# A new order for the token-only end of a two-layer metaformer kernel, with the FFN's fp8 casts on GpSimd

## The chip, the cores and the metric

The kernel runs on one core of a Trainium2 chip. A core has five engines with queues of their own: TensorE (PE, matrix products), VectorE (DVE), ScalarE (ACT), GpSimd (POOL) and SyncE (SP, which issues the transfers here). Each works through its own queue in order and waits for the others by semaphores. The metric is the device time of one execution in microseconds (us). One tick, below, is one turn of the kernel's main loop.

## The reference

The input `x` is 8 images of 128 x 128 pixels with 96 channels, in f32. Two layers follow one another. Each layer does

```python
x = x + conv(layernorm(x))      # eps 1e-6
t = x as tokens
t = t + ffn(layernorm(t))       # eps 1e-5
```

`conv` is a spectral filter: a product with `w1` to 192 channels, a squared ReLU, a two-dimensional real FFT, a product with a filter that is mixed for each image out of three learned ones by a small gate, the inverse FFT, and a product with `w2` back to 96 channels.

`ffn` is where the change is. With `q_mul` rounding to fp8 (5 exponent bits, 2 mantissa bits, overflow to infinity) and `q_acc` rounding to f16:

```python
def _qlinear(x, W, b):
    y = q_acc(jnp.einsum('bsk,nk->bsn', q_mul(x), q_mul(W)))
    return q_acc(y + q_mul(b))
h = jax.nn.relu(_qlinear(x, W1, b1))    # 96 -> 384
y = _qlinear(h, W2, b2)                 # 384 -> 96
```

So the normalised tokens are cast to fp8, the 384 hidden values are rounded to f16, biased, cut at zero and cast to fp8 again before the second product.

## The kernel before

The 2 x 8 pairs of layer and image are 16 jobs, and each job is cut into 16 groups, so every stage runs 256 groups (`n = NRG * len(jobs)`). There are four stages, written as Python generators whose `yield`s cut them into steps:

- `P`, `pixels`: loads 8 rows of pixels, normalises, multiplies by `w1`, squares, and does the first Fourier transform, along the width; the result goes to DRAM.
- `G`, `gate`: once per image, the mix of the three filters.
- `F`, `frequencies`: the transform along the height for 4 columns of frequencies, the filter, the product with `w2`, the inverse along the height; to DRAM.
- `S`, `tokens`: the inverse along the width for 8 rows, the residual, the layernorm, the FFN, the second residual, the store.

A fifth entry, `N`, does the small arithmetic of the layernorms: step 0 on VectorE (variance), step 1 on ScalarE (a logarithm and an exponential, for the inverse root), step 2 on VectorE (a refinement, and the bias of the normalisation).

No scheduler decides the order. A loop over ticks `t` walks through a tuple written by hand; an entry `(stage, step, ahead)` lets that step of the group `t - offset[stage] + ahead` be issued, with offsets 0 for P and G, 19 for F and 40 for S. Three tuples take turns: `RAMP` at the start, `TICK` for the body, and `TAIL` from the tick on at which only tokens are left (`t > n + offset["F"]`, that is from t = 276). At t = 276 the step with `ahead` 0 belongs to group 236, so some 20 groups of tokens remain for the tail. Each engine gets its instructions in the order of the tuple, and the loop goes on for as many ticks after the last group as the deepest step of `TAIL` lies behind (`last`). PSUM is four double banks, and `BANKS` and `TAIL_BANKS` say which tile takes which.

The steps of `tokens`, by number, with the name of the tile that the profile shows and the line in the kernel before:

| step | engine | what |
|---|---|---|
| 0 | SP | loads `v` (L742) and the residual `xr` (L744), 3 and 5 buffers |
| 1 | PE | `ps_r`, inverse transform (L748) |
| 2 | DVE | `xr` += `ps_r` (L757), 8 `bn_stats` (L371) |
| 3, 4 | DVE, ACT | normalise rows 0 to 3 and rows 4 to 7 into `xn_c`, fp8 (L772 on DVE, L766 on ACT) |
| 5 | PE | `pt_c`, 8 transposes (L780) |
| 6 | ACT | `xq`, the transposed tokens to SBUF (L783) |
| 7, 11, 15 | PE | `pm0`, `pm1`, `pm2`: a third of the 384 hidden values each (L790) |
| 8, 12, 16 | ACT | `y16`, `pm` to f16 (L793) |
| 9, 13, 17 | DVE | `a16`, bias and ReLU in f16 (L796) |
| 10, 14, 18 | ACT or POOL | `h8`, the fp8 cast of `a16` (L800 on ACT, L802 on POOL) |
| 19 | PE | `po`, second product, 24 matmuls (L807) |
| 20, 21 | ACT, DVE | `o16`, to f16 (L816), plus the bias (L818) |
| 22 | POOL, SP | `y` = `xr` + `o16` (L821), the store (L822) |

Which half of the rows ScalarE normalises is in `NORM_ACT`: `(1,)` means rows 4 to 7. Which of the three casts ScalarE makes is in `CAST_ACT`: `(0, 1, 2)` means all, and those that are not in it go to GpSimd.

Of the kernel before, what the change touches and what calls it, by code (L numbers as in the profile page):

```python
# [40 lines left out]
LAG = 3  # L41
WE = M + SC

NORM_ACT = (1,)
CAST_ACT = (0, 1, 2)
XS_ACT = (0, 1)


# [21 lines left out]
)  # L70

TAIL = (
    ("S", 5, -1), ("S", 14, -2), ("S", 15, -2), ("S", 6, -1), ("S", 2, 0), ("S", 7, -1),
    ("S", 16, -2), ("S", 19, -3), ("N", 0, 0), ("S", 8, -1), ("N", 1, 0), ("S", 20, -3),
    ("S", 17, -2), ("S", 9, -1), ("N", 2, 0), ("S", 3, 0), ("S", 21, -3), ("S", 10, -1),
    ("S", 11, -1), ("S", 22, -4), ("S", 12, -1), ("S", 0, 1), ("S", 1, 1), ("S", 4, 0),
    ("S", 13, -1), ("S", 18, -2),
)


# [6 lines left out]
    "pm1": 0, "pm2": 1, "po": 3, "pf2": 2, "py2": 0, "pz2": 2,  # L87
}
TAIL_BANKS = {
    "ps_r": 3, "pt_c": 1, "pm0": 1, "pm1": 2, "pm2": 2, "po": 3,  # L90
}

LAYER_INS = (
# [74 lines left out]
def _bc_mid(ap, n):  # L168

    p, a = ap.shape  # L170
    return ap.unsqueeze(1).to_broadcast([p, n, a])
# [3 lines left out]
def metaformer_kernel(ctx: ExitStack, tc: tile.TileContext, x, cst, layers, out):  # L175
# [5 lines left out]
    pp = ctx.enter_context(tc.tile_pool(name="psum", bufs=1, space=PSUM))  # L181

    banks = dict(BANKS, ps_w=0)

    def bank2(name):
        return pp.tile([128, 2, 512], F32, name=name, tag=f"d{banks[name]}")
# [165 lines left out]
    def rows(ap, g):  # L352
        return ap.rearrange("w (s h) c -> w s h c", s=2)[:, :, g * RH : (g + 1) * RH, :]
# [385 lines left out]
    def tokens(jb, g):  # L739
        wt = jb.wt  # L740
        v = ab.tile([128, RH, 2, C], F32, name="v", bufs=3)
        nc.sync.dma_start(v, jb.y[:, g * RH : (g + 1) * RH])  # L742
        xr = ab.tile([128, 2, RH, C], F32, name="xr", bufs=5)
        nc.sync.dma_start(xr, rows(jb.src, g))  # L744
        yield
        pr = bank2("ps_r")
        for s in range(2):
            mm(  # L748
                pr[:, s, : RH * C].rearrange("p (h c) -> p h c", c=C),
                kt["idft"],  # L750
                v[:, :, s, :],
                start=True,
                stop=True,
            )
        yield
        xv = xr.rearrange("p s h c -> p s (h c)")
        nc.vector.tensor_tensor(xv, pr[:, :, : RH * C], xv, ALU.add)  # L757
        x8 = xr.rearrange("p s h c -> p (s h) c")
        nm = norms[-1].stats(1, x8)
        yield  # L760

        xn = ab.tile([128, RG, C], F8, name="xn_c")
        for h in range(2):
            for j in range(RH * h, RH * h + RH):
                if h in NORM_ACT:
                    nc.scalar.activation(  # L766
                        xn[:, j, :], x8[:, j, :], AF.Identity,
                        bias=nm.nb[:, 1, j : j + 1], scale=nm.rs[:, 1, j : j + 1],
                        saturate=False,
                    )  # L770
                else:
                    nc.vector.tensor_scalar(  # L772
                        xn[:, j, :], x8[:, j, :], nm.rs[:, 1, j : j + 1], nm.nb[:, 1, j : j + 1],
                        ALU.mult, ALU.add, saturate=False,
                    )
            yield
        pt = bank2("pt_c")[:C]
        for j in range(RG):
            o = pt[:, j // 4, (j % 4) * 128 : (j % 4 + 1) * 128]
            mm(o, xn[:, j, :], ident8, start=True, stop=True)  # L780
        yield
        xq = ab.tile([C, 2, 512], F8, name="xq")
        nc.scalar.activation(xq, pt, AF.Copy, saturate=False)  # L783
        yield
        h8 = ab.tile([128, 3, 1024], F8, name="h8")
        for k in range(3):
            pm = bank2(f"pm{k}")
            fk = wt["f1_q"][:, k * 128 : (k + 1) * 128]
            for s in range(2):
                mm(pm[:, s, :], fk, xq[:, s, :], start=True, stop=True)  # L790
            yield
            y16 = ab.tile([128, 2, 512], F16, name="y16", bufs=3)
            nc.scalar.copy(y16, pm)  # L793
            yield
            a16 = ab.tile([128, 2, 512], F16, name="a16", bufs=3)
            nc.vector.tensor_scalar(a16, y16, wt["b1"][:, k : k + 1], 0.0, ALU.add, ALU.max)  # L796
            yield
            hk = h8[:, k, :].rearrange("p (a b) -> p a b", a=2)
            if k in CAST_ACT:
                nc.scalar.activation(hk, a16, AF.Copy, saturate=False)  # L800
            else:
                nc.gpsimd.tensor_copy(hk, a16, saturate=False)  # L802
            yield
        po = bank2("po")
        for j in range(RG):
            for k in range(3):
                mm(  # L807
                    po[:, j // 4, (j % 4) * C : (j % 4 + 1) * C],
                    h8[:, k, j * 128 : (j + 1) * 128],
                    wt["f2_q"][:, k, :],  # L810
                    start=k == 0,
                    stop=k == 2,
                )
        yield
        o16 = ab.tile([128, RG, C], F16, name="o16")
        nc.scalar.copy(o16.rearrange("p (a b) c -> p a (b c)", a=2), po[:, :, : RH * C])  # L816
        yield
        nc.vector.tensor_tensor(o16, o16, _bc_mid(wt["b2"], RG), ALU.add)  # L818
        yield
        y = ab.tile([128, 2, RH, C], F32, name="y")  # L820
        nc.gpsimd.tensor_tensor(y.rearrange("p s h c -> p (s h) c"), x8, o16, ALU.add)  # L821
        nc.sync.dma_start(rows(jb.dst, g), y)  # L822
        yield
# [6 lines left out]
    jobs = [Job(l, b) for l in range(len(layers)) for b in range(B)]  # L830
    first, last = max(a for _, _, a in RAMP), -min(a for _, _, a in TAIL)
    at, given, norms = {}, {}, []
    n = NRG * len(jobs)

    def advance(stage, step, last):

        for i in range(given.get((stage, step), 0), last + 1):
            if (stage, i) not in at:
                if stage == "N":
                    at[stage, i] = norms[i].steps()  # L840
                else:
                    at[stage, i] = stages[stage](jobs[i // NRG], i % NRG)
            next(at[stage, i])
            given[stage, step] = i + 1

    offset["N"] = -first
    with tc.manual_schedule():
        for t in range(-first, n + offset["S"] + last + 1):
            norms.append(Norms())
            if t < offset["F"] - 4:  # L850
                order, places = RAMP, RAMP_BANKS
            elif t > n + offset["F"]:
                order, places = TAIL, TAIL_BANKS
            else:
                order, places = TICK, BANKS
            banks.update(places)
            for stage, step, ahead in order:
                i = t - offset[stage] + ahead
                advance(stage, step, i if stage == "N" else min(i, n - 1))
# [40 lines left out]
```

## Time and profile before

| | before |
|---|---|
| time, median of 3 runs | 5379.85 us (5355.16 to 5381.69) |
| span of the profiled execution | 5367.8 us |
| TensorE, VectorE, ScalarE, GpSimd busy | 95%, 83%, 82%, 49% |
| mean granted TensorE clock | 0.974 of full speed |
| last `y` of the body's order (L821) | starts at 5134.6 us |
| last `y` of all | starts at 5362.5 us |

A line of a group reads: line, engine, operation, what is written from what, the sizes (partitions x elements) and types, how many; then, after the bar, the busy time in us and the mean of one in ns; then the time that the engine sat idle just before such instructions and what ended it. Busy time counts overlapping instructions once, so it can be less than the number times the mean. In the timeline, a line starts with the start in us and the duration in us.

The tail is the last 230 us or so of 5368, about 4% of the execution. It is the only part in which the instructions of the two kernels differ.

### The profile page before, as it was taken

Reading aid. Unit: us, or ns where it says so; the run is one execution under the profiler, and the core shown is the slowest. Engines: PE = TensorE matmul, PEld = TensorE weight load, DVE = VectorE, ACT = ScalarE, POOL = GpSimd, SP = SyncE. Lnnn points to the kernel's source line nnn. Section 1 sums busy time; section 2 is a strip of 40 time slices with the busy share of each in tenths; the row PEclk is TensorE's granted clock in tenths of the full one; section 3 lists DMA queues with packets and bytes.
Section 4 is the critical chain, followed back from the end, with each engine's and each line's share of the span. In section 5 each row is a group of like instructions: output and inputs, shape, how many; then the busy total and the mean of one; then the engine's idle time right before and its main releaser. Section 6 shows DMA issues by size and latency. Waiting matters only on the chain.

```text
span 5367.8 us, 116350 instructions
## 1 busy us (share of the span) xinstructions
PE 5075.2 (95%) x41192; PEld 4013.8 (75%) x41192; DVE 4474.8 (83%) x13814; ACT 4420.0 (82%) x7149; POOL 2651.8 (49%) x1911
## 2 busy tenths in 40 slices
PE   4899999999999999999999999999999999999876
PEld 2577777878787787878778787877878787787753
DVE  3887888888888888888888888888888888888876
ACT  2754688989898898989889898988989898897788
POOL 0355555555555555555555555555555555554421
PEclk7999999999999999999999999999999999999987
DMA  5566677777677777767777676777777677776643
GB/s 145 164 161 161 179 202 197 207 194 211 184 208 197 201 203 194 210 181 208 204 196 208 189 208 191 208 203 201 203 194 212 184 207 203 198 200 177 179 124 108
DMA packets 908040, 1020.14 MB, mean 190 GB/s; under 512 B 67106, under 2 KB 839954, under 8 KB 907122
## 3 DMA queue, kind: packets, MB, share of 16 engines
q1 hardware_dynamic: 907460, 1012.71, 68.3%
q8 instruction: 327, 5.36, 0.4%
q14 instruction: 253, 2.07, 0.1%
HBM read 598.62 MB, written 413.84 MB: 189 GB/s over the span
## 4 chain that ended last, share of the span: by engine, by line
PE 76%; DVE 8%; issue 6%; POOL 4%; ACT 3%; DMA 1%; SPq 1%; POOLq 0%; DVEq 0%; ACTq 0%
PE pw L458 13%; PE py L629 13%; PE pf L616 7%; PE pz L705 7%; PE pz L700 6%; PE pa L488 6%; PE pi L719 6%; PE ps_r L748 5%; PE pm L790 5%; PE pt_a L447 4%; PE po L807 3%; PE pt_c L780 2%; POOL ut L596 1%; DVE pr L647 1%; POOL y L821 1%
## 5 line engine op out<-in xcount | busy, mean ns | idle before, releaser
L659 POOL TENSOR_TENSOR xf<-pr 128x768 f32<-128x768 f32 (+2 forms) x544 | 957.0, 1762 | 312.5 <-DVE pr L651 278.0
L821 POOL TENSOR_TENSOR y<-xr,o 128x768 f32<-128x768 f32 x256 | 458.8, 1792 | 976.4 <-DVE o L818 940.8
L458 PE MATMUL pw<-w,xT 97*128 97x240 f32 x4096 | 925.1, 369 | 13.2 <-ACT xT L450 12.0
L443 POOL TENSOR_TENSOR xn_a<-xt,n_rs 128x768 f32<-128x768 f32 x256 | 413.6, 1616 | 976.8 <-DVE n_rs L409 852.8
L647 DVE TENSOR_TENSOR pr<-py,cf 128x768 f32<-128x768 f32 (+2 forms) x544 | 502.4, 924 | 465.6 <-PE py L629 422.8
L458 PEld LDWEIGHTS pw<-w,xT 97*128 97x128 f32 x4096 | 765.4, 192 | 136.4 <-ACT xT L450 22.8
L629 PE MATMUL py<-k_fwd,al 128*128 128x128 f32 x6272 | 838.9, 283 | 0.0
L793 ACT CAST y<-pm 128x1024 f16<-128x1024 f32 x768 | 770.8, 1005 | 58.3 <-PE pm L790 57.5
L800 ACT ACTIVATE h<-a 128x1024 fp8e5<-128x1024 f16 x768 | 808.3, 1055 | 0.4 <-DVE a L796 0.4
L629 PEld LDWEIGHTS py<-k_fwd,al 128*128 128x128 f32 x6272 | 751.1, 193 | 42.4 <-issue 7.3
L461 ACT ACTIVATE r<-pw 128x960 f32<-128x960 f32 x512 | 495.9, 969 | 280.1 <-PE pw L458 273.1
L596 POOL TENSOR_TENSOR ut<-ut,rw 112x768 f32<-112x768 f32 (+1 forms) x256 | 489.0, 1910 | 327.9 <-DMA ut<-u_d 177.7
L700 PE MATMUL pz<-w2b,xf 128*128 128x192 f32 (+1 forms) x2112 | 553.9, 344 | 8.8 <-DVE hr L534 5.0
L790 PE MATMUL pm<-xq,f_q 96*128 96x512 fp8e5 x1536 | 472.9, 390 | 71.7 <-ACT xq L783 39.7
L700 PEld LDWEIGHTS pz<-w2b,xf 128*128 128x128 f32 (+1 forms) x2112 | 337.7, 190 | 184.6 <-issue 143.1
L796 DVE TENSOR_SCALAR a<-y,b 128x1024 f16<-128x1024 f16 x768 | 434.2, 565 | 46.5 <-ACT y L793 46.5
L616 PEld LDWEIGHTS pf<-k_rh,ut 48*128 48x128 f32 x6272 | 376.8, 189 | 124.8 <-issue 65.1
L616 PE MATMUL pf<-k_rh,ut 48*128 48x128 f32 x6272 | 432.4, 284 | 36.9 <-POOL ut L596 35.8
L636 ACT COPY cf<-pf 128x768 f32<-128x768 f32 (+2 forms) x544 | 400.1, 796 | 36.2 <-PE pf L616 36.2
L465 ACT ACTIVATE xs<-r 128x768 f32<-128x768 f32 x512 | 427.6, 835 | 0.6
L783 ACT ACTIVATE xq<-pt_c 96x1024 fp8e5<-96x1024 f32 x256 | 260.7, 1018 | 184.0 <-PE pt_c L780 184.0
L719 PE MATMUL pi<-zt,k_inv 128*128 128x384 f32 (+1 forms) x1024 | 407.6, 522 | 0.0
(124 smaller groups left out, 10577.4 us busy)
## 6 DMA issues: line engine op xcount, KB each, us to landing
a_d<-at SPq DMA_DIRECT2D x256, 768.0 KB
al<-a_d SPq DMA_DIRECT2D x960, 192.0 KB
v<-y_d SPq DMA_DIRECT2D x256, 384.0 KB
y_d<-yt SPq DMA_DIRECT2D x480, 192.0 KB
ut<-u_d SPq DMA_DIRECT2D x240, 336.0 KB
xt<-in_x_dram SPq DMA_DIRECT2D x512, 96.0 KB
xr<-in_x_dram SPq DMA_DIRECT2D x128, 384.0 KB
mid<-y SPq DMA_DIRECT2D x128, 384.0 KB
```

What stands on the lines that cost most here:

```text
L458: mm(o, xT[:, 4 * a + 2 * i + j, :], wt["w1"], start=True, stop=True)
L596: nc.gpsimd.tensor_tensor(ut[:, :n], ut[:, :n], _bc_mid(jb.rw, n), ALU.mult)
L616: mm(pf[:nm, i, t * 128 : (t + 1) * 128], utf[64 * i : 64 * i + NHS, cs], kt["rh"][64 * i : 64 * i + NHS, :], start=True, stop=True,)
L629: mm(py[:nm, t, e, :], alf[:, e, cs], kt["fwd"][:, e, :], start=True, stop=True)
L647: nc.vector.tensor_tensor(p0, yq, crb, ALU.mult)
L659: nc.gpsimd.tensor_tensor(xv[:q, te], pr[:q, 0, te].rearrange("p t r k -> p t (r k)"), pr[:q, 1, te].rearrange("p t r k -> p t (r k)"), AL ...
L700: mm(o[:, : u * C], xf[:kb, 1, e, :], wt["w2b"][:kb, : u * C], start=True, stop=False,)
L719: mm(pi[:, e, : n * C], kt["inv"][:, e, :], zt[:, e, : n * C], start=True, stop=True)
L790: mm(pm[:, s, :], fk, xq[:, s, :], start=True, stop=True)
L793: nc.scalar.copy(y16, pm)
L800: nc.scalar.activation(hk, a16, AF.Copy, saturate=False)
L821: nc.gpsimd.tensor_tensor(y.rearrange("p s h c -> p (s h) c"), x8, o16, ALU.add)
```

## The change

From the tick on at which only tokens are left, GpSimd makes the three fp8 casts of the FFN instead of ScalarE, and ScalarE normalises all eight rows, of which VectorE did four. The order of the tail and its PSUM banks are written anew to go with it: for a group, `xq` now follows in the same tick as its normalisation, the residual and the statistics of a group are made one tick earlier, the pieces of a group lie at most three ticks apart and no longer four, and `pm0` and `pm1` share a bank while `pt_c` has one of its own. The purpose is to take work off ScalarE in the tail, where GpSimd has little to do. Before the tail, the two kernels issue the same instructions. What is computed is the same.

```diff
--- before.py
+++ after.py
@@ -41,8 +41,10 @@
 LAG = 3
 WE = M + SC
 
-NORM_ACT = (1,)
-CAST_ACT = (0, 1, 2)
+
+
+NORM_ACT, NORM_ACT_TAIL = (1,), (0, 1)
+CAST_ACT, CAST_ACT_TAIL = (0, 1, 2), ()
 XS_ACT = (0, 1)
 
 
@@ -70,11 +72,11 @@
 )
 
 TAIL = (
-    ("S", 5, -1), ("S", 14, -2), ("S", 15, -2), ("S", 6, -1), ("S", 2, 0), ("S", 7, -1),
-    ("S", 16, -2), ("S", 19, -3), ("N", 0, 0), ("S", 8, -1), ("N", 1, 0), ("S", 20, -3),
-    ("S", 17, -2), ("S", 9, -1), ("N", 2, 0), ("S", 3, 0), ("S", 21, -3), ("S", 10, -1),
-    ("S", 11, -1), ("S", 22, -4), ("S", 12, -1), ("S", 0, 1), ("S", 1, 1), ("S", 4, 0),
-    ("S", 13, -1), ("S", 18, -2),
+    ("N", 1, -1), ("S", 16, -2), ("S", 19, -3), ("N", 2, -1), ("S", 7, -1), ("S", 20, -3),
+    ("S", 8, -1), ("S", 1, 1), ("S", 17, -2), ("S", 21, -3), ("S", 9, -1), ("S", 18, -2),
+    ("S", 3, 0), ("S", 22, -3), ("S", 10, -1), ("S", 4, 0), ("S", 11, -1), ("S", 2, 1),
+    ("S", 12, -1), ("N", 0, 0), ("S", 5, 0), ("S", 6, 0), ("S", 13, -1), ("S", 14, -1),
+    ("S", 0, 2), ("S", 15, -1),
 )
 
 
@@ -87,7 +89,7 @@
     "pm1": 0, "pm2": 1, "po": 3, "pf2": 2, "py2": 0, "pz2": 2,
 }
 TAIL_BANKS = {
-    "ps_r": 3, "pt_c": 1, "pm0": 1, "pm1": 2, "pm2": 2, "po": 3,
+    "ps_r": 3, "pt_c": 1, "pm0": 0, "pm1": 0, "pm2": 2, "po": 3,
 }
 
 LAYER_INS = (
@@ -181,6 +183,7 @@
     pp = ctx.enter_context(tc.tile_pool(name="psum", bufs=1, space=PSUM))
 
     banks = dict(BANKS, ps_w=0)
+    on_act = {}
 
     def bank2(name):
         return pp.tile([128, 2, 512], F32, name=name, tag=f"d{banks[name]}")
@@ -762,7 +765,7 @@
         xn = ab.tile([128, RG, C], F8, name="xn_c")
         for h in range(2):
             for j in range(RH * h, RH * h + RH):
-                if h in NORM_ACT:
+                if h in on_act["norm"]:
                     nc.scalar.activation(
                         xn[:, j, :], x8[:, j, :], AF.Identity,
                         bias=nm.nb[:, 1, j : j + 1], scale=nm.rs[:, 1, j : j + 1],
@@ -796,7 +799,7 @@
             nc.vector.tensor_scalar(a16, y16, wt["b1"][:, k : k + 1], 0.0, ALU.add, ALU.max)
             yield
             hk = h8[:, k, :].rearrange("p (a b) -> p a b", a=2)
-            if k in CAST_ACT:
+            if k in on_act["cast"]:
                 nc.scalar.activation(hk, a16, AF.Copy, saturate=False)
             else:
                 nc.gpsimd.tensor_copy(hk, a16, saturate=False)
@@ -830,6 +833,7 @@
     jobs = [Job(l, b) for l in range(len(layers)) for b in range(B)]
     first, last = max(a for _, _, a in RAMP), -min(a for _, _, a in TAIL)
     at, given, norms = {}, {}, []
+    on_act.update(norm=NORM_ACT, cast=CAST_ACT)
     n = NRG * len(jobs)
 
     def advance(stage, step, last):
@@ -851,6 +855,7 @@
                 order, places = RAMP, RAMP_BANKS
             elif t > n + offset["F"]:
                 order, places = TAIL, TAIL_BANKS
+                on_act.update(norm=NORM_ACT_TAIL, cast=CAST_ACT_TAIL)
             else:
                 order, places = TICK, BANKS
             banks.update(places)
```

## The prediction

> **What bounds the kernel now.** I read the page first: ScalarE 82%, VectorE 83%, TensorE 95%, GpSimd 49%, all averages over a body that the change leaves alone. The list TAIL is in force only once pixels, gate and frequencies have run out, so I went on to busy time by stretch for the last 221 us (columns: stretch, its length, then busy us and instructions for PE, PEld, DVE, ACT, POOL, then clock and DMA).
>
> ```profile
> 5147.00:5181.00 34.00, 24.08 (x138) 13.70 (x138) 23.10 (x88) 28.48 (x46) 5.04 (x3) 0.80 0.38 118
> 5181.00:5344.00 163.00, 112.47 (x717) 65.06 (x715) 124.34 (x460) 154.38 (x240) 27.83 (x17) 0.83 0.37 119
> 5344.00:5367.80 23.80, 11.19 (x84) 7.44 (x84) 5.60 (x8) 14.30 (x19) 6.54 (x4) 0.50 0.18 67
> ```
>
> In the middle stretch 17 token groups pass (17 POOL instructions, one y each), so a tick is 163/17 = 9.59 us. ScalarE is busy 154.4/163 = 95%, GpSimd 17%. The groups of that stretch say what fills ScalarE:
>
> ```profile
> L800 ACT ACTIVATE h<-a 128x1024 fp8e5<-128x1024 f16 x52 | 53.0, 1051 | 0.0
> L793 ACT CAST y<-pm 128x1024 f16<-128x1024 f32 x52 | 51.3, 1005 | 1.4 <-PE pm L790 1.2
> L766 ACT ACTIVATE xn_c<-xr,n_nb,n_rs 128x96 fp8e5<-128x96 f32 x68 | 26.2, 463 | 0.0
> L783 ACT ACTIVATE xq<-pt_c 96x1024 fp8e5<-96x1024 f32 x17 | 17.1, 1007 | 0.0
> L816 ACT CAST o<-po 128x768 f16<-128x768 f32 x17 | 13.5, 794 | 6.7 <-PE po L807 6.6
> L796 DVE TENSOR_SCALAR a<-y,b 128x1024 f16<-128x1024 f16 x51 | 37.9, 743 | 33.9 <-ACT y L793 33.9
> L772 DVE TENSOR_SCALAR xn_c<-xr,n_rs,n_nb 128x96 fp8e5<-128x96 f32 x68 | 17.8, 325 | 0.6
> ```
>
> The fp8 casts (L800) are ScalarE's largest item. It idles only 0.5 us a tick, mostly for po; the others wait for it. So ScalarE bounds the tail.
>
> The a16 step deserves a second look: the groups give it 743 ns, but its own view has a median of 480 and a maximum of 5401, and the timeline shows why.
>
> ```profile
> L796 DVE TENSOR_SCALAR a<-y,b x768: 470/480/5401, 636.2 to 5356.9; 128x1024 f16<-128x1024 f16 x192
> ...
> 5314.99 1.64 POOL L821 TENSOR_TENSOR y<-xr,o 128x768 f32<-128x768 f32 x1 [8.32 <-DVE o L818]
> 5315.86 1.05 DVE L796 TENSOR_SCALAR a<-y,b 128x1024 f16<-128x1024 f16 x1 [0.95 <-ACT y L793]
> ```
>
> It began while GpSimd's y ran and ended at 5316.91, 0.28 us after y. VectorE had to wait for GpSimd to finish.
>
> **What the Trainium skill says.** "SBUF — State Buffer", section "Who interferes with whom": VectorE and GpSimd share one port pair as an exclusive lock; a VectorE instruction in a two-port mode, or with two SBUF inputs, and a GpSimd instruction exclude each other for their whole length, and ScalarE waits for nobody. The pair of lines above agrees. "GPSIMD Engine Reference", section 4.1 "Engine selection", calls one-input work "roughly line-rate"; section 3.1 says the best tight loop takes about 1.8 cycles an element at 1.2 GHz. These two give different prices for the cast; the rows below speak for the first.
>
> **The change, part by part.**
>
> *Price of a GpSimd cast.* The trace has none of f16 to fp8. The nearest rows, from the GpSimd groups by form:
>
> ```profile
> L589 POOL MEMSET al<- 64x384 f32 x16 | 6.8, 423 | 0.9
> L472 POOL COPY acc<-r 128x192 f32<-128x192 f32 x16 | 5.5, 341 | 12.0 <-ACT r L461 12.0
> L332 POOL MEMSET pad<- 65x3072 f32 x1 | 2.7, 2658 | 0.0
> ```
>
> The memsets give (2658 - 423)/(3072 - 384) = 0.83 ns an element. The copy of 192, extended by 832 elements at 0.83, gives 341 + 692 = 1.03 us. At 1.8 cycles (1.5 ns) it would be 1.59 us; with the whole 341 ns put on the elements, 1.82 us. I take 1.04 us because the trace's slope is a measured one, and keep 1.04 to 1.8 for the range. That fp8 output costs nothing extra is an assumption.
>
> *ScalarE.* Its instructions overlap a little: the groups add up to 168.3 us (with 7.2 us for L399 and L400) against 154.4 busy, a factor of 0.917. Three casts leave: 53.0/17 x 0.917 = 2.86 us a tick. Four more row normalisations arrive, as many as it does now: 26.2/17 x 0.917 = 1.41 us. From 154.4/17 = 9.08 us, ScalarE falls to 7.63 us a tick.
>
> *VectorE* loses 17.8/17 = 1.05 us of normalising, some 6 us being left: not the bound by itself.
>
> *GpSimd* goes from 1.64 to 1.64 + 3 x 1.04 = 4.76 us: not the bound by itself either.
>
> *The shared port.* This is what the change loads. Its users in a tick: GpSimd's y 1.64 and three casts 3.12; VectorE's three a16 of 0.48 = 1.44, the o16 add 0.55, the five small statistics operations of N step 0 0.86 (5319.22 to 5320.08 in the timeline) and the five of N step 2 0.72. Together 8.33 us, of which little overlaps. And the new order lines them up: GpSimd's queue is cast 2, y, cast 0, cast 1; VectorE's is N2, a16(2), o16 add, a16(0), xr add and statistics, N0, a16(1). N0 must wait for cast 0, then a16(1) releases cast 1, which holds N2, behind which stand a16(2), the o16 add and a16(0), for which cast 2 and y wait, and after y comes cast 0 again. Some 0.1 to 0.2 us of start-up is hidden in the waits, about as much goes to semaphores. I take 8.3 us.
>
> *The new waits, and who queues behind.* xq of a group now follows its normalising in the same tick: one y16 evacuation (1.0 us) lies between, and the last transposes end some 0.5 us after the last row, so this is hidden. po waits for GpSimd's cast 2 of the tick before, which is over half a tick old. In the steady tick o16 waits for po: from the last normalised row TensorE does pt_c (0.5), pm (0.6 to 1.0), po (2.1) while ScalarE does y16, xq, Ln and Exp, y16 (3.3 us), so a stall of about 0.1 to 0.3 us, no worse than the 0.4 of now. The banks: pm0 and pm1 share one, but between them lie y16(0) and eight rows (2.9 us); pt_c has its own. Nothing.
>
> *Loads.* xr has five buffers, so the load of group g+2 waits for y of g-3, and the SyncE queue holds v behind the store of that y. Now v is issued at 5307.35 and ps_r uses it at 5314.02. In the new order y comes later in the tick and ps_r earlier: about 4 us are left, and the bursts at 5308 to 5311.6 show all three transfers done in under 4. Just hidden, I say.
>
> *Ends.* The deepest step goes from 4 ticks behind to 3, but the last group still has its own chain (pm, y16, a16, cast, po, o16, y), and the cast there is no faster. I give start and end together 0.
>
> *Sum.* The tick falls from 9.59 to 8.3, by 1.29 us. Nineteen ticks lie between the first whole tail group (236) and the last (255): 19 x 1.29 = 24.5 us. 5379.85 - 25 = 5355 us.
>
> **The rivals.** (A) The above, the port at 8.3 us: 5355.
> (B) ScalarE stays the bound because GpSimd slips between VectorE's instructions: 7.63 + 0.2 = 7.8 us, 19 x 1.79 = 34, so 5346. For it: small statistics operations have gaps between them. Against: those ten are dependent and each needs the port.
> (C) The cast takes 1.6 us: port 5.22 + 4.8 = 10.0 us, at best 9.6 with what overlaps: 0 to +8 us, 5380 to 5388. For it: the skill's 1.8 cycles. Against: the copy row, which would leave only 53 ns for its start.
> (D) The cast takes 1.8 us or more, as fp8 might by a slower path: 10.6 us and above, 19 x 1.0 or more: 5400 and up, slower than before.
> (E) The loads come late by half a microsecond or so: tick 8.9, 19 x 0.7 = 13, so 5367.
>
> **How the numbers follow.** A 0.50, B 0.20, C 0.12, D 0.08, E 0.10. Half a per cent is 27 us, a bound at 5353, so A is split by 0.2 us of tick: 0.24 faster, 0.26 same. B goes to faster: 0.44. Same gets E and 0.05 of C: 0.41. Slower: 0.07 of C and D: 0.15. The three times of before span 5355 to 5382, so the measurement adds some 10 us each way. Low 5335 is B less that; high 5388 is the top of C. Outside stay D and some of B.
>
> **What would show it.** After: L800's successor on GpSimd at about 1.04 us; ScalarE's rows at eight a group; y every 8.3 us; VectorE's a16 and N0 lengthened by waiting for GpSimd, and ScalarE busy about 92%. A cast of 1.5 us or more makes A and B wrong; a ScalarE idle before y16 or xn for lack of v or xr means E; ticks of 7.8 mean B. Before 5147 us nothing should differ.

## The result, and the profile after

The changed kernel took 5330.35 us (median of 4 runs, 5329.69 to 5336.65) beside 5376.11 us for the kernel before on the same chip (4 runs, 5355.16 to 5381.69): a ratio of 0.9925 with a 95% interval of 0.9896 to 0.9953. Two more comparisons of the same pair gave 0.9929 [0.9906, 0.9953] and 0.9941 [0.9928, 0.9954]. It is faster, by 0.6 to 0.75%, some 32 to 46 us. As a time, 5330.35 lies 5 us below the low end of the predicted range; as a ratio on the 5379.85 us that the prediction started from, it is 5339.5 us and inside.

One figure of the table above has to be corrected before anything is compared. The `y` that starts at 5134.6 us belongs to group 231. The last `y` of the body's order is that of group 233, and it starts at 5161.6 us, so the part that the new order rules is the last 206 us of the kernel before and not 230.

All lines after L41 moved by 2, later by 3: the fp8 cast is L805 on GpSimd and L803 on ScalarE, `a16` L799, `y16` L796, the normalised rows L769, `ps_r` L751, `y` L824, the first operation of N step 2 L406. Over the whole execution the engines' shares hardly changed (TensorE 95%, VectorE 84%, ScalarE 82%); GpSimd rose from 49% to 51%.

What counts is the tail. Here is its steady stretch in the busy time by stretch (the columns as in the prediction: PE, PEld, DVE, ACT, POOL, clock, DMA), and below it the groups of the same stretch:

```profile
5172.00:5314.00 142.00, 101.68 (x752) 59.10 (x751) 116.13 (x395) 135.28 (x267) 91.59 (x73) 0.90 0.44 140
```

```profile
L805 POOL CAST h<-a 128x1024 fp8e5<-128x1024 f16 x55 | 61.8, 1124 | 51.0 <-DVE a L799 51.0
...
L769 ACT ACTIVATE xn_c<-xr,n_nb,n_rs 128x96 fp8e5<-128x96 f32 x143 | 53.2, 466 | 0.0
...
L799 DVE TENSOR_SCALAR a<-y,b 128x1024 f16<-128x1024 f16 x54 | 34.7, 643 | 8.6 <-ACT y L796 8.0 <-ACT n_rs L402 0.3 <-issue 0.2
...
L406 DVE SCALAR_TENSOR_TENSOR n_a<-n_rs 128x8 f32<-128x8 f32 x17 | 14.9, 877 | 3.2 <-ACT n_rs L403 2.1
```

Eighteen groups now pass in 142 us, a tick of 7.89 us where it was 9.54 (the mean from the `y` of group 235 to that of 253, in each kernel). ScalarE makes eight rows a group (143 for 18 groups) and is still 135.3/142 = 95% busy, which invites the reading that it bounds the tail as before. Two rows speak against that. The first operation of N step 2 (L406) works on 8 elements a partition and takes 877 ns on the mean, and `a16` takes 643 where its shortest took 470: VectorE stands and waits inside these instructions. Alone this proves little, since `a16` took 743 in the kernel before, where ScalarE was the bound. The experiments decide which of the two it is.

The tail by its marks, all from GpSimd's timeline; "tail" is from the start of the `y` of group 233 to the end of the span, "tick" the mean from group 235 to 253:

| | `y` of 233 starts | tail | tick |
|---|---|---|---|
| before | 5161.6 us | 206.2 us | 9.54 us |
| after | 5153.6 | 174.2 | 7.89 |
| after, two more profiles | 5153.2, 5179.9 | 177.0, 174.5 | 7.99, 7.85 |

The last tick of the mean is a short one in most kernels (7.15 us in the changed one), since the work is running out by then; "shortest tick" below leaves it out.

So the tail itself gave 29 to 32 us. In the first pair 18 ticks x (9.54 - 7.89) = 29.8 us account for it, and the tail's two ends for the other 2. The other 8 us of the first pair of profiles lie ahead of the tail, where the instructions are the same. In 14 profiles of this case, one of them of the kernel before, the `y` of group 233 starts anywhere between 5146 and 5180 us, so the 8 us are taken as scatter and not as an effect of the change.

### The profile page after: what moved, and what is told of

It is laid out like the page before. It is cut to its first block, busy times and chain, and to the rows that moved or that the text cites. A ratio compares the mean times of both kernels' runs of the same rounds, so it can differ in the third digit from the quotient of the medians.

```text
span 5327.8 us, 116431 instructions
## 1 busy us (share of the span) xinstructions
PE 5054.9 (95%) x41192; PEld 4001.1 (75%) x41192; DVE 4455.7 (84%) x13738; ACT 4386.9 (82%) x7163; POOL 2724.6 (51%) x1973
## 4 chain that ended last, share of the span: by engine, by line
PE 78%; DVE 8%; ACT 4%; issue 3%; POOL 3%; DMA 2%; SPq 1%; POOLq 0%; DVEq 0%; ACTq 0%
PE pw L461 14%; PE py L632 13%; PE pf L619 7%; PE pz L708 7%; PE pz L703 6%; PE pa L491 6%; PE pi L722 6%; PE ps_r L751 5%; PE pm L793 5%; PE pt_a L450 4%; PE po L810 4%; PE pt_c L783 2%; POOL ut L599 1%; DVE pr L650 1%; DVE st L374 1%
## 5 line engine op out<-in xcount | busy, mean ns | idle before, releaser
L824 POOL TENSOR_TENSOR y<-xr,o 128x768 f32<-128x768 f32 x256 | 462.8, 1808 | 803.2 <-DVE o L821 769.1
L796 ACT CAST y<-pm 128x1024 f16<-128x1024 f32 x768 | 771.7, 1005 | 58.9 <-PE pm L793 58.3
L803 ACT ACTIVATE h<-a 128x1024 fp8e5<-128x1024 f16 x706 | 745.1, 1055 | 0.2 <-DVE a L799 0.2
L799 DVE TENSOR_SCALAR a<-y,b 128x1024 f16<-128x1024 f16 x768 | 422.3, 550 | 11.1 <-ACT y L796 10.5
L751 PE MATMUL ps_r<-v,k_idft 128*128 128x384 f32 x1024 | 394.0, 508 | 36.1 <-DMA v<-y_d 22.6
L769 ACT ACTIVATE xn_c<-xr,n_nb,n_rs 128x96 fp8e5<-128x96 f32 x1100 | 422.9, 467 | 0.0
```

What stands on the lines that cost most here:

```text
L751: mm(pr[:, s, : RH * C].rearrange("p (h c) -> p h c", c=C), kt["idft"], v[:, :, s, :], start=True, stop=True,)
```

## The experiments

Two theories stood at the start. T1 (P, later V, in the expectations below): the turn is VectorE's, work plus waits for the port that it shares with GpSimd, and ScalarE is only nearly as long. T2 (S): ScalarE is still the bound (7.63 us by the prediction) plus small stalls. Beside both stood the question which of the three parts of the change, engines, order and banks, brings the gain.

### The parts by themselves: order_only, engines_only, casts_only, banks_old

`order_only` keeps the new order and banks and the engines of before; `engines_only` keeps the engines and takes back order and banks; `casts_only` moves the casts in the new order but leaves rows 0 to 3 on VectorE; `banks_old` takes back the banks alone.

```diff
order_only
-NORM_ACT, NORM_ACT_TAIL = (1,), (0, 1)
-CAST_ACT, CAST_ACT_TAIL = (0, 1, 2), ()
+NORM_ACT, NORM_ACT_TAIL = (1,), (1,)
+CAST_ACT, CAST_ACT_TAIL = (0, 1, 2), (0, 1, 2)
casts_only
-NORM_ACT, NORM_ACT_TAIL = (1,), (0, 1)
+NORM_ACT, NORM_ACT_TAIL = (1,), (1,)
engines_only: TAIL and TAIL_BANKS of before
banks_old
-    "ps_r": 3, "pt_c": 1, "pm0": 0, "pm1": 0, "pm2": 2, "po": 3,
+    "ps_r": 3, "pt_c": 1, "pm0": 1, "pm1": 2, "pm2": 2, "po": 3,
```

> The new order and banks alone; ScalarE keeps the three casts and normalises rows 4 to 7 as before. Theory S (ScalarE is what bounds the tail, before and after): its work stays at 9.08 us a tick, so the tick can fall only by its idle time, from 9.55 to 9.1 to 9.5, and the kernel lies within 8 us of the one before. Theory O (the order brought most of it): tick 8.3 or less, and most of the 40 us are there without moving any work.

> The old order and banks, with all rows normalised on ScalarE and all casts on GpSimd. Theory S with an order that does not matter: ScalarE's work is 7.5 us a tick, tick 7.7 to 8.1, 28 us or more faster than before. If the new order is needed for the move: the old order puts the second product and the transposes closer behind what they need, so waits come up, tick 8.5 to 9.3 and only 5 to 20 us faster than before.

> The changed kernel, but VectorE normalises rows 0 to 3 again, as before the change. Theory S: ScalarE falls from 7.5 to 6.1 us a tick, so the tick falls below 7.89, to 7.0 to 7.6, until the next wait ends last. Theory P (the port that VectorE and GpSimd share bounds the tail): its users' time grows by the 1.05 us of normalising, tick 8.4 to 9.0, slower than the changed kernel by 10 to 20 us.

> The changed kernel with the PSUM banks of the tail as before, in which pt_c shares one with pm0 and pm1 one with pm2. pm0 of a group then waits for xq of the next group's predecessor as before, and pt_c for the y16 that reads pm0, which stands well before it on ScalarE; pm1 waits for the y16 of pm2, half a tick before. I expect little: tick 7.9 to 8.3, 0 to 8 us slower than the changed kernel. If the banks are a large part of the gain: 9 us or more a tick.

| | time | ratio to before | tail | tick |
|---|---|---|---|---|
| order_only | 5383.85 us | 1.0026 [1.0018, 1.0035] | 220.4 us | 10.11 us |
| engines_only | 5467.04 | 1.0178 [1.0152, 1.0204] | 301.5 | 14.16 |
| casts_only | 5383.18 | 1.0025 [1.0016, 1.0033] | 219.2 | 10.20 |
| banks_old | 5336.72 | 0.9941 [0.9919, 0.9963] | 174.1 | 7.82 |

Neither the order with its banks nor the move of work gains anything alone, and order and casts without the rows gain nothing either; only the banks don't matter. The rows without the casts were not run. `banks_old` came out beside its expectation. `order_only` and `casts_only` came out slower than either theory had them, P having only the sign right for `casts_only`, and `engines_only` lost where both expectations had a gain.

`order_only`, busy time by stretch and then its waits (engine and what waited, for whom: us in all, times, the longest):

```profile
5185.00:5300.00 115.00, 84.44 (x468) 46.61 (x466) 86.81 (x305) 103.86 (x161) 18.78 (x12) 0.80 0.36 114
```

```profile
ACT h L803 <- DVE a L799: 11.0, 23, 0.8
```

ScalarE has 103.9 us of work in 115/10.15 = 11.3 ticks, 9.2 us a tick as before, and waits 11.0 us, 0.97 a tick, for the `a16` that the new order puts shortly ahead of two of its three casts. 9.2 + 0.97 gives the tick of 10.15. The order is made for a cast that sits on another engine.

`engines_only` falls into a loop. In the order of before, `y` of an old group stands behind the first cast of the group three later in GpSimd's queue. The longest wait and a piece of the timeline:

```profile
PE ps_r L751 <- DMA v<-y_d: 63.4, 8, 8.6
```

```profile
5259.56 1.63 POOL L824 TENSOR_TENSOR y<-xr,o 128x768 f32<-128x768 f32 x1
...
5261.22 0.56 SPq L825 DMA_DIRECT2D out_dram<-y  x1
...
5261.87 0.56 SPq L745 DMA_DIRECT2D v<-y_d  x1
...
5266.39 2.90 PE L751 MATMUL ps_r<-v,k_idft 128*128 128x384 f32 x4 [7.96 <-DMA v<-y_d]
```

The cast waits for `a16` (it starts at 5258.55, 0.14 us after that ends), `y` for the cast, the store for `y`, the load of `v` for the store in the same SyncE queue, `ps_r` 4.5 us later for `v`, and what stands behind `ps_r` in TensorE's queue and behind the `xr` addition in VectorE's, down to the next such `a16`, for `ps_r`. One turn of this loop takes some 15 us (5259.56 to the next `y` at 5274.75); the 14.16 of the table holds the shorter ticks at its end.

`casts_only` shows why ScalarE has to take all rows. Its stretch, and the rows on VectorE from its groups:

```profile
5185.00:5300.00 115.00, 73.16 (x465) 44.97 (x464) 109.28 (x303) 70.71 (x124) 56.91 (x45) 0.84 0.36 114
```

```profile
L775 DVE TENSOR_SCALAR xn_c<-xr,n_rs,n_nb 128x96 fp8e5<-128x96 f32 x44 | 34.0, 831 | 0.0
```

ScalarE is 61% busy, VectorE 95%. A row on VectorE took 325 ns before and takes 831 beside GpSimd's `y` and casts. The four rows of a group take 3.09 us together (5219.31 to 5222.40), the time in which `y` and cast 0 run; cast 0 ends at 5221.86. The `xr` addition and the statistics, which have that place in the changed kernel and lose nothing there (see the next part), come after them: 7.31 + 3.0 is the tick of 10.3 that this kernel keeps. ScalarE's rows in the same stretch stay at 471 (463 before). This is what the Trainium skill states on the page "SBUF — State Buffer", section "Who interferes with whom": the lock is between VectorE and GpSimd, and ScalarE waits for nobody. The measured rows agree.

### Who sets the turn: extra_cast, half_norm

`extra_cast` makes the cast of `k = 0` a second time on GpSimd. `half_norm` leaves the normalising of rows 0 to 3 out, so that ScalarE has 1.4 us a tick less to do; TensorE transposes rows 4 to 7 twice instead.

```diff
extra_cast
             else:
                 nc.gpsimd.tensor_copy(hk, a16, saturate=False)
+                if k == 0:
+                    nc.gpsimd.tensor_copy(hk, a16, saturate=False)
half_norm (half: in the tail)
             for j in range(RH * h, RH * h + RH):
+                if half and h == 0:
+                    continue
...
-            mm(o, xn[:, j, :], ident8, start=True, stop=True)
+            mm(o, xn[:, RH + j % RH if half else j, :], ident8, start=True, stop=True)
```

> The changed kernel, with the first of the three casts of each token group made twice on GpSimd, writing the same values: 1.04 us more of GpSimd and of the shared port a tick. Theory S: GpSimd idles 2.8 us a tick, so the tick rises by at most 0.3 us, the kernel by 0 to 6 us. Theory P: the tick rises by the whole 1.04 us, the kernel by about 20 us.

> The changed kernel, but in the tail only rows 4 to 7 are normalised, on ScalarE, and their tokens stand in for those of rows 0 to 3: half of the normalising is left out. ScalarE's work falls by 1.4 us a tick to 6.1, and no other engine's rises. Theory S: tick 6.5 to 7.0, 17 us or more less. Theory P or L (the port, or the loads, set the tick): the tick stays above 7.5.

`extra_cast` took 5346.45 us (0.9958 [0.9944, 0.9973]); the mean tick is 8.22 us and the shortest 8.11. `half_norm` took 5344.57 us (0.9962 [0.9949, 0.9974]): with less work on ScalarE it is no faster than the changed kernel. Its stretch of 18 ticks:

```profile
5187.00:5333.00 146.00, 98.38 (x752) 59.16 (x751) 118.97 (x395) 111.01 (x195) 92.02 (x73) 0.85 0.42 136
```

ScalarE is 111/146 = 76% busy, and the shortest tick is 7.31 us, exactly the shortest of the changed kernel. So ScalarE's 95% did not set it. T2 falls. Most of the other ticks of `half_norm` are about 9 us long, and what makes long ticks is the matter of the next part.

Where the 7.31 us come from can be read off one turn of VectorE and GpSimd in the changed kernel's timeline (start, duration; in brackets idle time ahead and what ended it):

```profile
5181.16 1.81 POOL L824 TENSOR_TENSOR y<-xr,o 128x768 f32<-128x768 f32 x1
...
5181.39 0.94 DVE L760 TENSOR_TENSOR xr<-ps_r,xr 128x768 f32<-128x768 f32 x1
...
5182.37 1.38 DVE L374 BATCH_NORM_STATS2 st<-xr 128x6 f32<-128x96 f32 x8
...
5182.91 1.03 POOL L805 CAST h<-a 128x1024 fp8e5<-128x1024 f16 x1
...
5184.58 0.48 DVE L799 TENSOR_SCALAR a<-y,b 128x1024 f16<-128x1024 f16 x1
...
5185.12 1.04 POOL L805 CAST h<-a 128x1024 fp8e5<-128x1024 f16 x1 [1.18 <-DVE a L799]
...
5185.39 0.78 DVE L406 SCALAR_TENSOR_TENSOR n_a<-n_rs 128x8 f32<-128x8 f32 x1 [0.33 <-ACT n_rs L403]
...
5186.65 0.48 DVE L799 TENSOR_SCALAR a<-y,b 128x1024 f16<-128x1024 f16 x1
...
5187.05 0.55 DVE L821 TENSOR_TENSOR o<-o,b 128x768 f16<-128x768 f16 x1
5187.20 1.30 POOL L805 CAST h<-a 128x1024 fp8e5<-128x1024 f16 x1 [1.03 <-DVE a L799]
...
5187.98 0.80 DVE L799 TENSOR_SCALAR a<-y,b 128x1024 f16<-128x1024 f16 x1 [0.38 <-ACT y L796]
5188.47 1.81 POOL L824 TENSOR_TENSOR y<-xr,o 128x768 f32<-128x768 f32 x1
```

From `y` to `y` it is 7.31 us. VectorE meets GpSimd twice. L406 ends at 5186.17, 0.01 after cast 1 (5186.16); alone it takes 0.17. The `a16` at 5187.98 ends at 5188.78, 0.28 after cast 2 (5188.50); alone it takes 0.48. The two meetings cost 0.61 and 0.32 us and the idle time just ahead of them is 0.33 and 0.38, 1.6 us in all; the other 5.7 of the turn are VectorE's own instructions, which overlap a little (each at its length alone, they add up to 6.0). That idle time costs nothing in itself: were ScalarE sooner, the instruction would start sooner and still end behind the cast. On the other side, `y` and cast 0 run beside the `xr` addition and the statistics, and VectorE loses nothing there.

In `extra_cast` a third meeting appears, in N step 0 (its groups):

```profile
L398 DVE SCALAR_TENSOR_TENSOR n_v<-n_d 128x8 f32<-128x8 f32 x17 | 10.9, 640 | 0.6
```

It takes 640 ns instead of 167, and the first operation of that step 328 instead of 183. The shortest tick rises by 8.11 - 7.31 = 0.80 us for a cast of 1.04: in such a tick the meeting's cost comes through, less what is hidden. The mean tick rises by only 8.22 - 7.89 = 0.33 and the tail by 6 to 9 us, which is nearer to what S foretold (at most 0.3, and 0 to 6 us) than to P's 1.04 and 20. The trace says why: where `ps_r` comes late, VectorE waits for it ahead of the `xr` addition (0.79 us in the tick of 8.40 from 5225.23), gets to N step 0 when the second cast is nearly over, and the third meeting costs it 0.24 us in place of 0.80. So T1 holds for the short ticks; the long ones have another cause.

### The long ticks: after_rep, loads_first, loads_first_rep, after_rep2

Eleven of the 18 ticks of the changed kernel are longer than 7.31 us, 7.6 to 9.1. Its waits name the loads, and one engine further on `ps_r` itself:

```profile
PE ps_r L751 <- DMA v<-y_d: 22.6, 12, 2.5
DVE xr L760 <- PE ps_r L751: 9.4, 10, 1.7
```

In twelve of 18 ticks TensorE waited for `v`, 22.6 us in all. VectorE waited for `ps_r` in ten, 9.4 us in all, or 0.52 a tick, and that is nearly the whole of 7.89 - 7.31. Not all of it is the load's, however. One of these ticks:

```profile
5226.24 2.81 PE L751 MATMUL ps_r<-v,k_idft 128*128 128x384 f32 x4 [1.78 <-DMA v<-y_d]
...
5229.09 0.96 DVE L760 TENSOR_TENSOR xr<-ps_r,xr 128x768 f32<-128x768 f32 x1 [1.26 <-PE ps_r L751]
```

The same four matmuls took 1.56 us a tick later, at 5234.49. TensorE's granted clock was 1.00 there and 0.52 here. Set against 1.56 us, the slow `ps_r` make up about 5.0 of the 9.4 us (an estimate from the seven of them in these ticks, 1.74 to 2.90 us long); the late start makes up the rest. In the two other profiles of the changed kernel it is 6.5 of 11.2 and 4.5 of 8.8.

`loads_first` moves the loads: step 0 of group g+2 comes first in the order instead of near the end, and in the tail `xr`, which needs the buffer that `y` frees, is loaded one step after `v`, so that `v` does not wait for that buffer. In SyncE's queue `v` still stands behind a store of `y`, but behind that of one group earlier, so it goes out nearly a tick sooner before its use. `after_rep` and `after_rep2` are the changed kernel again; `loads_first_rep` repeats `loads_first` beside the latter.

```diff
 TAIL = (
+    ("S", 0, 2),
     ("N", 1, -1), ("S", 16, -2), ...
-    ("S", 0, 2), ("S", 15, -1),
+    ("S", 15, -1),
...
+        tail = not on_act["cast"]
+        if tail:
+            yield        # between the loads of v and xr
...
-        yield
+        if not tail:
+            yield
```

> The changed kernel once more. The stretch before the tail holds the same instructions in both kernels, and in the two first profiles it differed by 8 us, so I expect the tail alone, 32 us or 0.6%: a ratio of 0.994, and from the y of group 233 to the end 172 to 177 us, with a tick of 7.8 to 8.0 us.

> The changed kernel with the load of v at the head of the tail's order and that of xr one tick later, so that SyncE's queue no longer holds a load of v behind a store that waits for y. Theory L (in part of the ticks the inverse transform waits for v, 22.6 us in all, and that sets the longer ticks): every tick becomes as short as the short ones, 7.3 to 7.5 us, and the kernel is 7 to 10 us faster than the changed one. If that wait is beside the work that counts: tick 7.8 to 8.0, no difference.

> The changed kernel a third time, beside the version with the early loads. Its tail should again take 172 to 177 us from the y of group 233 on. If the stretch before the tail, where the instructions are those of before, is shorter in it by something lasting, that y comes at 5153 us again and the ratio is 0.993; if that was chance, anywhere from 5146 to 5169, and the ratio nearer to 0.994.

> The early loads a second time, for the comparison with the changed kernel: tick 7.4 to 7.6 us, 167 to 170 us from the y of group 233 to the end, 6 to 9 us less than the changed kernel in the tail. In the whole time that is 0.1 to 0.15%, which the scatter before the tail may hide.

| | time | ratio to before | tail | tick |
|---|---|---|---|---|
| after_rep | 5332.07 us | 0.9929 [0.9906, 0.9953] | 177.0 us | 7.99 us |
| loads_first | 5329.39 | 0.9931 [0.9905, 0.9957] | 168.1 | 7.49 |
| after_rep2 | 5341.90 | 0.9941 [0.9928, 0.9954] | 174.5 | 7.85 |
| loads_first_rep | 5331.52 | 0.9925 [0.9912, 0.9938] | 167.6 | 7.52 |

In `loads_first` no wait of `ps_r` for `v` is left; what it waits for is its bank, which `o16` reads (at most 1.4 us). `ps_r` takes 1.56 us in every tick (in all but two in `loads_first_rep`), and VectorE no longer waits for it. So early loads took away both parts of the wait, the late start and the slow `ps_r`: 7.89 - 7.49 = 0.4 us a tick, and the tail shortens by 6 to 9 us. The granted clock of the stretch is 0.96 to 0.97 in the two profiles with early loads and 0.88 to 0.91 in the three of the changed kernel (5172 to 5310 us). Why it is higher is not shown; no run moves the clock alone. In the total the gain is of the size of its scatter: 2.7 us between the medians of the first pair, 10.4 of the second, and the intervals of the ratios overlap. The tail's marks show the gain, the whole time only suggests it. It is the best version that was found. Its stretch shows what is next:

```profile
5176.00:5310.00 134.00, 99.28 (x744) 56.72 (x744) 112.70 (x394) 132.91 (x265) 90.57 (x72) 0.97 0.45 145
```

ScalarE is now 132.9/134 = 99% busy: it has no room below 7.4 us, just above VectorE's turn of 7.31.

### Below both bounds: loads_half, loads_half_cast2

`loads_half` is `loads_first` with rows 0 to 3 left out as in `half_norm`, so that VectorE's turn alone should remain. `loads_half_cast2` takes the same kernel and moves cast 2 back to ScalarE, which has room for it, to take one meeting away from VectorE.

```diff
loads_half: the edits of loads_first and half_norm together
loads_half_cast2: and (the test for the tail goes by NORM_ACT_TAIL there)
-CAST_ACT, CAST_ACT_TAIL = (0, 1, 2), ()
+CAST_ACT, CAST_ACT_TAIL = (0, 1, 2), (2,)
```

> The early loads together with half of the normalising left out (in the tail only rows 4 to 7 are normalised, their tokens stand in for those of rows 0 to 3). Theory V (with the loads on time, VectorE's own turn with its two waits for the port sets the shortest tick): tick 7.3 to 7.4, as the shortest ticks of all the kernels with three casts on GpSimd, though ScalarE then works only 6.1 us a tick. Theory S (ScalarE): 6.2 to 6.9 us.

> The same, half of the normalising left out, and the third cast made by ScalarE again: ScalarE works 7.0 us a tick, and the port has one user less, so that VectorE no longer waits for that cast before its first a16 of a group. Theory V: more work for ScalarE, and yet a shorter tick, 7.0 to 7.2 us, ScalarE's own. If the 7.31 us come from TensorE or from the chain through PSUM: the tick stays at 7.3 or rises.

`loads_half` took 5327.5 us (0.9929 [0.9908, 0.9950]), tail 168.4, mean tick 7.51. Without the last, shortened one there are 17 ticks: eight of 7.31 to 7.34, five of 7.5 to 7.7 and four of 8.1 to 8.4, with ScalarE at 90.1/110 = 82%:

```profile
5190.00:5300.00 110.00, 76.19 (x593) 45.69 (x593) 98.45 (x330) 90.12 (x161) 73.26 (x59) 0.89 0.45 145
```

With ScalarE unloaded and the loads out of the way, the floor of the tick is still 7.31, and in such a tick VectorE hardly idles. From the `xr` addition at 5170.31 to the next at 5177.63 both meetings are there, the first operation of N step 2 taking 1.01 us behind cast 1, and the only idle time marked on VectorE is the 0.16 us ahead of the second:

```profile
5176.68 1.02 DVE L807 TENSOR_SCALAR a<-y,b 128x1024 f16<-128x1024 f16 x1 [0.16 <-ACT y L804]
```

ScalarE is busy for 6.15 us of this turn and TensorE for 4.63. So the floor is VectorE's turn, with its waits for the port. The four longest ticks are those in which VectorE waits for `ps_r`:

```profile
DVE xr L765 <- PE ps_r L756: 3.4, 4, 1.0
```

`ps_r` takes 2.65 to 2.93 us in them, at a granted clock of 0.50 to 0.56, though `v` is on time. Because of them the mean of the 17 ticks, 7.61 us, is no better than the 7.51 of `loads_first`. Without these four it is 7.42, so ScalarE's 99% costs `loads_first` some 0.1 us a tick (an estimate from these means).

`loads_half_cast2` missed what was expected. It took 5340.53 us (0.9947 [0.9928, 0.9966]), and every tick but the shortened last is 8.10 to 8.13 us: one GpSimd instruction of 1.04 us fewer, and the turn is 0.8 us longer. A tick that rises had been named beforehand as the sign that TensorE or the chain through PSUM sets the floor. The trace speaks against these two: here too the only idle time marked on VectorE in a turn is 0.16 us, ahead of `a16`. The timeline shows the meeting that replaced the old one:

```profile
5221.92 1.64 POOL L832 TENSOR_TENSOR y<-xr,o 128x768 f32<-128x768 f32 x1 [1.52 <-DVE o L829]
5222.00 1.85 DVE L807 TENSOR_SCALAR a<-y,b 128x1024 f16<-128x1024 f16 x1 [0.16 <-ACT y L804]
```

Without cast 2 in front of it, `y` starts as soon as the `o16` addition is done, at the very moment at which VectorE comes to `a16` of the next group. That `a16` now waits for a `y` of 1.64 us and lasts 1.85, where in `loads_half` it waited for a cast and lasted 1.02. 1.85 - 1.02 = 0.83 is, within 0.02, the difference of the ticks (8.12 - 7.31).

## Why the prediction was right, and where its sum was not

The direction, the mechanism and the order of size were right; the port's term was too large, two terms that were put at nothing were not, and it is luck that these errors partly cancelled. By its steps:

- *Price of a GpSimd cast.* Forecast 1.04 us. Measured, the line view of L805:

```profile
L805 POOL CAST h<-a x62: 1028/1040/1304, 5161.6 to 5318.7; 128x1024 fp8e5<-128x1024 f16 x62
```

  The median of 1040 ns is the figure taken, so rivals C and D fall. The Trainium skill's "roughly line-rate" for one-input work ("GPSIMD Engine Reference", section 4.1) was the nearer of its two statements. Nothing extra for fp8 output shows, though no cast to f16 was timed beside it. The mean of 1124 holds casts of 1.30 us, which waited for VectorE's `o16` addition in their turn.
- *ScalarE.* Forecast 7.63 us a tick, measured 135.3/18 = 7.52. Right.
- *VectorE, GpSimd by themselves.* Neither is a bound by work alone; VectorE becomes one with its waits, as step "shared port" said.
- *The shared port.* The step "Together 8.33 us, of which little overlaps", which was taken as 8.3, is the first term that was mis-sized: the turn is 7.31 us. So about 1.0 us does overlap. A blocked instruction ended 0.01 to 0.28 us after the one it waited for, so its start-up lay in the wait; and VectorE spends the length of `y` and cast 0 in the `xr` addition and the statistics, which were not in the port's sum and do not stop for GpSimd. What holds is the chain of two meetings that the step described (cast 1 before N2, cast 2 before `a16`). The third that it named, N0 behind cast 0, hardly came: the statistics last until cast 0 is nearly over, and N0's first operation ended 0.04 us after it. What failed is adding up durations of all the port's users as if they stood in one line.
- *Loads.* "Just hidden" is the second. TensorE waited for `v` in 12 of 18 ticks, and the late start of `ps_r` cost VectorE about (9.4 - 5.0)/18 = 0.24 us a tick. This was rival E's mechanism, which was weighed at 0.10 and on top of a tick of 8.3.
- *TensorE.* The third has no place in the sum: the time of `ps_r` was taken as free. At a granted clock near one half it takes up to 2.90 us instead of 1.56, which cost VectorE about 5.0/18 = 0.28 us a tick. Early loads took 0.4 us of the two together off the tick.
- *New waits, banks.* Nothing, as forecast: `banks_old` has the tick (7.82) and the ratio of the changed kernel within their scatter. ScalarE waited for `po` once in 142 us, 0.6 us.
- *Ends.* Forecast 0. From the `y` of 233 to that of 235 it is 19.5 us before and 18.5 after; from the `y` of 253 to the end 14.9 and 13.7. Two us in all: small, as taken.
- *Sum.* 18 ticks x (9.54 - 7.89) = 29.8 us and 2 from the ends, against the 24.5 forecast from 19 ticks; the errors, -1.0 us a tick for the port and +0.5 for the waits for `ps_r`, partly cancelled, and the tick of 7.89 came out beside rival B's 7.8 for another reason than B's: GpSimd does not slip between VectorE's instructions, and ScalarE is not the bound in the short ticks. That the mean lies where B put it is chance too.
- *Faster or same.* The prediction's split laid a little more on faster; three ratios of 0.9925 to 0.9941 put the gain just beyond half a per cent.

## What to carry to other kernels

Moving work from a full engine to an idle one paid here only together with an order that places the instructions of VectorE and GpSimd against each other: the same move in the old order cost 1.8%, and in the new one it gained 0.6 to 0.75%. To find the bound of a steady loop, walk one turn and mark each instruction that lasts longer than its shortest: an engine at 95% was not the bound of the short turns, and one at 82% was. Ask of every load which store stands ahead of it in its queue, since the one in front waits for the end of another group.

## What the hardware showed that was not expected

- A wait for the shared port is counted inside the waiting instruction. The 128x8 operation L406 lasts 0.17 us alone and 0.78 to 1.0 us behind a cast; `a16` lasts 0.48 alone, 0.8 to 1.2 behind a cast and 1.85 behind `y`. So "busy" on VectorE contains waiting.
- Which GpSimd instruction is met weighs more than how much GpSimd does: with a cast of 1.04 us taken off GpSimd, the shortest tick went from 7.31 to 8.10 us, since `a16` met the 1.64 us of `y` instead.
- The load of `v`, issued at 5261.87 right behind the store of `y`, released its matmul at 5266.39, 4.5 us later, while the whole turn of the faster kernel is 7.31 us.
- TensorE's granted clock reached the tick although TensorE was only 72% busy in the changed kernel's stretch: the four matmuls of `ps_r` took 1.56 us at a clock of 1.00 and 2.92 at 0.50 (`loads_half`), and VectorE waited for the slow ones.
